# The exchange through DRAM: rows of its blocks at a pitch of 5 KB

## The chip, the cores and the metric

The kernel runs on one core of a Trainium2 chip. The core has a matrix engine (TensorE, PE in the profile, with its weight loads as PEld), a vector engine (VectorE, DVE), a scalar engine (ScalarE, ACT), GpSimd (POOL) and SyncE (SP), which here does nothing but issue DMAs. Sixteen DMA engines move data between DRAM (HBM) and the on-chip memory SBUF, which has 128 partitions. The metric is the device time of one execution in microseconds, as the median of several runs; lower is better.

## What is computed

One block of a transformer with a mixture of experts, in float32: 16 sequences of 256 tokens, 256 features, 16 heads of 64, and 8 experts with 1024 hidden units. Cut to what matters:

```python
shift = silu(t) @ W_ada.T + b_ada
h = _ln(x, ln1_g, ln1_b) + shift
qkv = (h @ Wqkv.T).reshape(b, n, 3, H, HD)
q = _ln(qkv[:, :, 0].transpose(0, 2, 1, 3), qn_g, qn_b)
k = _ln(qkv[:, :, 1].transpose(0, 2, 1, 3), kn_g, kn_b)
v = qkv[:, :, 2].transpose(0, 2, 1, 3)
attn = softmax(einsum('bhnd,bhmd->bhnm', q, k) / sqrt(HD), axis=-1)
o = einsum('bhnm,bhmd->bhnd', attn, v).transpose(0, 2, 1, 3).reshape(b, n, H * HD)
x = x + o @ Wout.T
tok = x.reshape(-1, d)
gate = softmax(tok @ Wgate.T, axis=-1)
vals, idx = top_k(gate.T, tok.shape[0] // E)      # each expert takes 512 tokens
g = _ln(tok[idx.T.reshape(-1)], mlp_g, mlp_b).reshape(-1, E, d)
y = gelu(einsum('ked,ehd->keh', g, fc1s) + b1s)
y = (einsum('keh,edh->ked', y, fc2s) + b2s) * vals.T[..., None]
tok = tok.at[idx.T.reshape(-1)].add(y.reshape(-1, d))
```

## The kernel before

The attention part goes through the 16 sequences one after another, with the work of neighbours overlapped. For each sequence the class `First` (L632) normalises x and turns it, and `Group` (L676) multiplies it with `wqkvT` in six groups of 512 columns for each half of 128 tokens. Groups 0 and 1 are queries, 2 and 3 keys, 4 and 5 values. `Quad` (L796) is the attention of four heads in two pairs (index `i`): scores, row maxima, exponentials with row sums, division by the sums, and the product with v. `Tail` (L918) projects with `woutT`, adds x, stores the tokens and their normalised form, and works out the gate. After the last sequences comes the routing and then the expert part (`Job`, L1190), which loads 2 MB of weights for each job.

Two things have to be transposed so that the contraction lies on the partitions: queries and keys (tokens on the partitions when they come out of the matmul, head features wanted there), and the probabilities (queries on the partitions, keys wanted). For the first and the last sequence (`DIRECT`, L171) TensorE transposes. For the fourteen others it is done by an exchange through DRAM, in four steps:

- `turn` (L751 for queries and keys, L846 for probabilities): VectorE transposes blocks of 32 x 32 in place, within each group of 32 partitions, into a tile of 128 partitions x 1024 floats (`kb` or `pb`, 4 KB in each partition).
- `away` (L759 and L856): one DMA on SP's queue writes the whole tile, 512 KB, to a tile in DRAM named `kblocks` or `blocks`, shape [4, 32, 4, 256], the row of 4 KB of each partition after that of the partition before. All these DRAM tiles share four buffers (`bufs=4`).
- `back` (L766 and L869): four DMAs on SP's queue read it, `q` = 0 to 3. Read `q` takes from each of the 128 rows the piece of 1 KB at place `q`, and writes 32 partitions of SBUF, four pieces into each: for probabilities to `prT`, for queries to `qraw`, for keys to `kT`.
- The consumer: ScalarE's `affine` (L777) applies gain and bias to queries (L781) and keys (L789), on which the scores (L813) wait; the product with v (L900) reads `prT` directly.

For a sequence with the exchange that makes 12 stores (four of queries and keys, eight of probabilities) and 48 reads.

The order of the instructions on every engine and on SP's queue is not found at run time. `Plan` (L45) collects steps, and a list of numbers written out by hand, `PLACES` (L182), sorts them; `PERIOD` (L173) is the distance of two sequences in those numbers, 48.3. A step that waits for a semaphore holds up everything behind it on the same engine. On SP, in particular, a `back` waits for the landing of its `away`, and later DMAs stand behind it. The durations given with the steps (`took`, `lag`) are notes; the order is that of `PLACES`.

Of the kernel before, what the change touches and what calls it, by code (L numbers as in the profile page):

```python
# [9 lines left out]
F32 = mybir.dt.float32  # L10
# [9 lines left out]
B, N, D = 16, 256, 256  # L20
# [14 lines left out]
SQ = 32  # L35
QB = P // SQ
# [28 lines left out]
def kernel(  # L65
# [17 lines left out]
    dram = ctx.enter_context(tc.tile_pool(name="dram", bufs=1, space=DRAM))  # L83
# [444 lines left out]
    if True:  # L528
# [147 lines left out]
        class Group:  # L676
# [80 lines left out]
                )  # L757

            def away(self, kb):  # L759
                self.blocks = dram.tile([QB, SQ, QB, N], F32, tag="blocks", bufs=4, name="kblocks")  # L760
                nc.sync.dma_start(
                    self.blocks.rearrange("k d q n -> (k d) (q n)"),
                    kb[0].rearrange("p q t h m -> p (q t h m)"),
                )

# [30 lines left out]
        class Quad:  # L796
# [58 lines left out]

            def away(self, i):  # L856

                self.blocks[i] = dram.tile([QB, SQ, QB, N], F32, tag="blocks", bufs=4, name="blocks")
                nc.sync.dma_start(
                    self.blocks[i].rearrange("k m q n -> (k m) (q n)"),  # L860
                    self.pb[i].rearrange("p q c h t n -> p (q c h t n)"),
                )

# [486 lines left out]
        for b in range(B):  # L1350
# [16 lines left out]
            for (g, t), p in GROUP.items():  # L1367
                p += base
                a = Group(b, g, t)
                n = (b, g, t)  # L1370
# [3 lines left out]
                if g < 4:  # L1374
# [4 lines left out]
                    if b not in DIRECT:  # L1379
                        kb, blocks = ("pb", b, -1, g), ("blocks", b, -1, g)  # L1380
# [17 lines left out]
            for d in range(HP // 2):  # L1398
# [3 lines left out]
                n = (b, d)  # L1402
                po = ("po", 0) + n
                for i in range(2):
                    q = p + 3 * i
                    m = n + (i,)
                    sums, pb, prT, blocks = ("sums",) + m, ("pb",) + m, ("prT",) + m, ("blocks",) + m
# [20 lines left out]
            for t in range(TB):  # L1428
                a = Tail(b, t)
                p = base + TAIL[t]  # L1430
                n = (b, t)
# [55 lines left out]
        for n in range(2):  # L1487
            a = jobs[n]
            k = top + 10 + 20 * n
# [4 lines left out]
            for i in range(6):  # L1494
                name, took, by = {"D": ("DVE", 0.81, nc.vector), "P": ("POOL", 1.4, nc.gpsimd), "A": ("ACT", 3.5, nc.scalar)}[who[i]]
# [13 lines left out]
        k = top + 30  # L1509
# [36 lines left out]
        for k in range(1, len(jobs)):  # L1546
# [4 lines left out]
            for s in range(SLOTS):  # L1551
# [28 lines left out]
                else:  # L1580
                    i, q = divmod(s - FC, 4)
# [56 lines left out]
```

## Time and profile before

| | |
|---|---|
| median of 3 runs | 1095.7 us (1095.66 to 1098.27) |
| profiled execution | 1098.53 us, its span 1096.8 us |
| TensorE busy | 1050.9 us (96% of the span) |
| VectorE busy | 809.8 us (74%) |
| GpSimd busy | 615.8 us (56%) |
| ScalarE busy | 591.5 us (54%) |
| DMA traffic | 238.56 MB in 167,700 packets |
| granted TensorE clock | 0.992 of full speed on average |

The span is the time from the first to the last instruction of the profiled execution. Busy times leave out register, branch, semaphore and DMA-issuing instructions. A line of a group or a wait names the engine, the tile that is written and the source line; "A <- B" means that A stood idle until B released it. Matmuls are pipelined, so the busy time of TensorE counts some overlapped time, and some of its stalls are not seen as idle. The DMA share is the time that packets took, summed over the 16 engines and divided by 16 times the length of the stretch; packets in flight can overlap on an engine, so it can be a little over 1. The attention part lasts until about 800 us and the routing and expert part from there to the end.

### The profile page before, as it was taken

The numbers are of one execution on the slowest core, as the hardware profiler recorded it, in microseconds if no ns is written. First come the engines' busy times: TensorE is split into PE (matmuls) and PEld (weight loads), VectorE is DVE, ScalarE is ACT, GpSimd is POOL, SyncE is SP. The second block draws the span as 40 slices with busy tenths as digits, with TensorE's granted clock in tenths as the row PEclk, the third lists the DMA queues.
The fourth block names the chain that finished last, engine by engine and source line by source line (L and its number), as shares of the span: only waits on it lengthen the run. The fifth ranks groups of instructions, "written<-read, shape, count | busy, mean of one in ns | idle before, by whom it ended". The sixth has DMA issues, their size and how long they took to land. (4 is left out here: it accounts for less than half of the span.)

```text
span 1096.8 us, 18716 instructions
## 1 busy us (share of the span) xinstructions
PE 1050.9 (96%) x5611; PEld 685.9 (63%) x5611; DVE 809.8 (74%) x2257; ACT 591.5 (54%) x1656; POOL 615.8 (56%) x997
## 2 busy tenths in 40 slices
PE   6999999999999999999999999999988999999996
PEld 3555646556454645555565555656667888888885
DVE  6667878888887797887888788875579488655540
ACT  1768666666665655666666557675622323332331
POOL 3766766678667585666667676665411333333332
PEclk8999999999999999999999999999999999999998
DMA  6026989999998999998999999986120456565661
GB/s 213 1 77 188 273 261 294 285 281 261 282 278 269 282 280 284 283 286 255 281 294 275 285 283 266 310 265 186 64 101 20 132 172 202 169 174 171 194 202 19
DMA packets 167700, 238.56 MB, mean 218 GB/s; under 512 B 17328, under 2 KB 139440, under 8 KB 167600
## 3 DMA queue, kind: packets, MB, share of 16 engines
q1 hardware_dynamic: 159680, 227.08, 70.2%
q0 software_dynamic: 6144, 8.39, 4.2%
q10 hardware_dynamic: 1776, 1.90, 0.5%
q8 instruction: 45, 0.74, 0.3%
q14 instruction: 55, 0.45, 0.2%
HBM read 136.64 MB, written 100.66 MB: 216 GB/s over the span
## 5 line engine op out<-in xcount | busy, mean ns | idle before, releaser
L688 PE MATMUL pm<-wq,hT 128*128 128x512 f32 x768 | 361.5, 606 | 13.1 <-DVE qk L721 6.3
L841 POOL TENSOR_SCALAR pr<-pr,sums 128x256 f32<-128x256 f32 x512 | 237.0, 481 | 107.3 <-DVE sums L837 99.5
L830 ACT ACTIVATE pr<-sc,nmax 128x256 f32<-128x256 f32 x512 | 237.3, 481 | 98.3 <-DVE nmax L821 78.6
L688 PEld LDWEIGHTS pm<-wq,hT 128*128 128x128 f32 x768 | 136.8, 190 | 168.1 <-issue 131.6
L103 POOL TENSOR_TENSOR ss<-ss,neghalf 128x8 f32<-128x8 f32 x128 | 211.0, 1648 | 10.6
L821 DVE TENSOR_REDUCE nmax<-sc 128x2 f32<-128x512 f32 x256 | 165.4, 673 | 19.9 <-PE sc L813 19.6
L851 DVE STREAM_TRANSPOSE pb<-pr 128x512 f32<-128x512 f32 x224 | 150.1, 690 | 20.7 <-DMA kblocks<-kb 9.5
L813 PE MATMUL sc<-kT,qT 64*128 64x256 f32 x1024 | 137.4, 396 | 3.5 <-ACT kT L789 3.0
L900 PE MATMUL po<-prT,v 128*64 128x256 f32 x1024 | 129.5, 387 | 2.1 <-DMA prT<-blocks 1.8
L701 ACT ACTIVATE sq<-pm 128x512 f32<-128x512 f32 x128 | 75.8, 604 | 96.1 <-PE pm L688 95.6
L813 PEld LDWEIGHTS sc<-kT,qT 64*128 64x128 f32 x1024 | 91.9, 186 | 52.8 <-issue 26.7
L1319 POOL DMA_INDIRECT out<-y,idx x32 | 51.2, 1599 | 119.1 <-DVE y L1313 65.9
L1286 PE MATMUL ph<-xT,w 128*128 128x256 f32 x512 | 117.8, 383 | 0.0
L1302 PE MATMUL py<-w,hid 128*128 128x256 f32 x512 | 116.3, 380 | 0.0
L926 PE MATMUL pw<-wo,oT 128*128 128x256 f32 x512 | 115.3, 382 | 0.0
L926 PEld LDWEIGHTS pw<-wo,oT 128*128 128x128 f32 x512 | 96.2, 190 | 20.9 <-issue 6.0
L830 ACT ACTIVATION_READ_ACCUMULATOR pr<-sc,nmax 128x1 f32 x512 | 109.0, 213 | 0.0
L900 PEld LDWEIGHTS po<-prT,v 128*64 128x64 f32 x1024 | 66.8, 136 | 67.1 <-issue 23.7
L705 DVE TENSOR_REDUCE ss<-sq 128x8 f32<-128x512 f32 x128 | 85.1, 671 | 29.1 <-ACT sq L701 28.6
L1293 ACT ACTIVATE hid<-ph,vec 128x256 f32<-128x256 f32 x128 | 60.3, 473 | 84.6 <-PE ph L1286 79.5
L1302 PEld LDWEIGHTS py<-w,hid 128*128 128x128 f32 x512 | 95.6, 190 | 12.8
L1286 PEld LDWEIGHTS ph<-xT,w 128*128 128x128 f32 x512 | 95.4, 190 | 12.8
(141 smaller groups left out, 1096.1 us busy)
## 6 DMA issues: line engine op xcount, KB each, us to landing
blocks<-pb SPq DMA_DIRECT2D x112, 512.0 KB, 5.0
prT<-blocks SPq DMA_DIRECT2D x448, 128.0 KB, 4.3
kblocks<-kb SPq DMA_DIRECT2D x56, 512.0 KB, 4.3
w<-in_fc2T SPq DMA_DIRECT2D x16, 1024.0 KB, 5.7
w<-in_fc1T SPq DMA_DIRECT2D x16, 1024.0 KB, 8.3
qraw<-kblocks SPq DMA_DIRECT2D x112, 128.0 KB, 4.0
kT<-kblocks SPq DMA_DIRECT2D x112, 128.0 KB, 4.2
out<-tok SPq DMA_DIRECT2D x32, 128.0 KB, 4.1
```

The lines of the kernel that those rows point to most:

```text
L103: nc.gpsimd.tensor_tensor(dst, src, neghalf[:, : src.shape[1]], ALU.pow)
L688: nc.tensor.matmul(self.pm, hTs[self.b][:, c, bass.ts(self.t, P)], wq[:, c, bass.ts(self.g, GW)], start=(c == 0), stop=(c == DC - 1),)
L705: nc.vector.tensor_reduce(self.ss[:, 0, :], self.sq.rearrange("p (h d) -> p h d", d=HD), AX.X, ALU.add,)
L813: nc.tensor.matmul(self.sc[i, j][:, t, :], qTs[self.b][rows, hp, bass.ts(t, P)], keys[rows, hp] if direct else keys[rows, hp // 4, hp % 4] ...
L821: nc.vector.tensor_reduce(self.nmax[i, j], self.sc[i, j], AX.X, ALU.max, negate=True)
L830: nc.scalar.activation(self.pr[i, j][:, t, :], self.sc[i, j][:, t, :], AF.Exp, bias=self.nmax[i, j][:, t : t + 1], scale=1.0, accum_out=se ...
L841: nc.gpsimd.tensor_scalar(self.pr[i, j][:, t, :], self.pr[i, j][:, t, :], self.sums[i][:, 1, j, t : t + 1], 1.0, ALU.mult, ALU.mult,)
L851: nc.vector.transpose(self.pb[i][:, :, :, j].rearrange("p k c t n -> p t k c n"), self.pr[i, j].rearrange("p t (k c m) -> p t k c m", c=TB ...
L900: nc.tensor.matmul(self.po[j * HD : (j + 1) * HD, i, :], vs[self.b][:, c, bass.ts(4 * self.d + 2 * i + j, HD)], prT[:, j, c] if self.b in ...
L926: nc.tensor.matmul(self.pw, oTs[self.b][:, hp // 2, self.t, hp % 2, :], wo[:, hp, :], start=(hp == 0), stop=(hp == HP - 1),)
L1286: nc.tensor.matmul(self.ph[f], self.w1[:, c, bass.ts(f, P)], self.xT[:, c, :], start=(c == 0), stop=(c == DC - 1),)
L1302: nc.tensor.matmul(self.py[i], self.hid[:, f, bass.ts(i, P)], self.w2[:, f, :], start=(f == 0), stop=(f == FC - 1),)
```

## The change

The DRAM tiles of the exchange get one more place along their third axis, five places of 256 floats where there were four. The stores write the first four, and the reads take the first four, as before. So the row of each partition still has 4 KB of data, but rows start 5 KB apart and the last 1 KB of each is never written or read. A tile takes 640 KB of DRAM rather than 512 KB. `back` is not touched: it indexes places 0 to 3 of the wider tile.

```diff
             def away(self, kb):
-                self.blocks = dram.tile([QB, SQ, QB, N], F32, tag="blocks", bufs=4, name="kblocks")
+                self.blocks = dram.tile([QB, SQ, QB + 1, N], F32, tag="blocks", bufs=4, name="kblocks")
                 nc.sync.dma_start(
-                    self.blocks.rearrange("k d q n -> (k d) (q n)"),
+                    self.blocks[:, :, :QB].rearrange("k d q n -> (k d) (q n)"),
                     kb[0].rearrange("p q t h m -> p (q t h m)"),
                 )
...
             def away(self, i):
 
-                self.blocks[i] = dram.tile([QB, SQ, QB, N], F32, tag="blocks", bufs=4, name="blocks")
+                self.blocks[i] = dram.tile([QB, SQ, QB + 1, N], F32, tag="blocks", bufs=4, name="blocks")
                 nc.sync.dma_start(
-                    self.blocks[i].rearrange("k m q n -> (k m) (q n)"),
+                    self.blocks[i][:, :, :QB].rearrange("k m q n -> (k m) (q n)"),
                     self.pb[i].rearrange("p q c h t n -> p (q c h t n)"),
                 )
```

## The prediction

> **What bounds the kernel now.** I read the page first, for the share of each engine, then the stretches of one period each, then the waits of TensorE and ScalarE, and last short stretches in which the DMA engines did one kind of work.
>
> The page's busy times, slices and DMA part:
>
> ```profile
> span 1096.8 us, 18716 instructions
> PE 1050.9 (96%) x5611; PEld 685.9 (63%) x5611; DVE 809.8 (74%) x2257; ACT 591.5 (54%) x1656; POOL 615.8 (56%) x997
> ...
> PE   6999999999999999999999999999988999999996
> ...
> DMA  6026989999998999998999999986120456565661
> ...
> q1 hardware_dynamic: 159680, 227.08, 70.2%
> ...
> blocks<-pb SPq DMA_DIRECT2D x112, 512.0 KB, 5.0
> prT<-blocks SPq DMA_DIRECT2D x448, 128.0 KB, 4.3
> kblocks<-kb SPq DMA_DIRECT2D x56, 512.0 KB, 4.3
> ```
>
> The reader is to see two rows of nines: TensorE from the second slice on, and the DMA engines in slices 5 to 26, which is the attention part. The exchange through DRAM (the last three lines, with the reads into qraw and kT) is most of the traffic: 168 stores of 512 KB and 672 reads of 128 KB, 88 MB each way, 176 of the 227 MB of the SP queue.
>
> One period (the work of one sequence) takes 48.2 us: the output projections of sequence 1 begin at 117.8 us and those of sequence 14 at 744.7, thirteen periods later. Stretches of about one period, with TensorE's busy time, its clock, the share of the 16 DMA engines and the rate:
>
> ```profile
> 158.00:206.00 48.00, 47.43 (x224) 1.00 0.96 276
> 302.00:350.00 48.00, 46.89 (x220) 1.00 0.93 268
> 446.00:494.00 48.00, 45.61 (x224) 1.00 1.02 289
> 638.00:686.00 48.00, 47.44 (x239) 1.00 1.00 284
> ```
>
> Thirteen such stretches, from 110 to 734 us, give a mean DMA share of 0.978 and 608.0 us of TensorE busy in 624. So both are nearly full, TensorE at full clock, and only 16.0 us of TensorE's idle time are left to win there. Where TensorE or its weight loads wait there for the exchange, it shows in these rows (total us, times, longest):
>
> ```profile
> PE sc L813 <- ACT kT L789: 3.0, 3, 1.9
> PE po L900 <- DMA prT<-blocks: 1.8, 3, 1.4
> ...
> PEld sc L813 <- ACT kT L789: 5.0, 4, 2.3
> PEld sc L813 <- ACT qT L781: 2.7, 4, 0.8
> ...
> ACT kT L789 <- DMA kT<-kblocks: 18.4, 16, 2.0
> ACT qT L781 <- DMA qraw<-kblocks: 11.7, 10, 2.3
> ```
>
> ScalarE waits for the reads of keys and queries for 30.1 us in all, and about 13.3 us of that reaches TensorE: 3.0 + 1.8 + 5.0 + 2.7, and 0.8 us of weight loads that wait for prT directly.
>
> **The change, part by part.** No instruction is added or removed; nothing moves on any queue. Per period there are still 12 stores (away, L759 and L856) and 12 groups of four reads (back, L766 and L869). Sizes stay: the trace's packet records show stores in packets of 4096 bytes and reads in packets of 1024, and each row of 4 KB and each piece of 1 KB stays contiguous. What changes is addresses: rows start every 5 KB, so the 128 pieces of one read, which all sat at the same offset within 4 KB, now step through all four offsets. A tile grows from 512 to 640 KB of DRAM, which nothing waits for.
>
> Issue. A store's DRAM side was one run of 512 KB and is now 128 rows with gaps, so its issue could cost more. A store issues in 338 to 376 ns (medians of the two lines), a read, with one more dimension, in 430. At worst 92 ns x 12 = 1.1 us of SP per period, and at best nothing. SP stands waiting 61.0 us for stores of probabilities to land in 110 to 734 us, 4.7 us a period, which covers it. I take 0; without the cover it would be 13 x 1.1 = 14 us at most.
>
> The reads. Three stretches, each with one kind of transfer only (columns: busy of the engines, clock, DMA share, GB/s):
>
> ```profile
> 335.00:339.00 4.00, 4.00 (x23) 1.94 (x23) 3.97 (x8) 1.95 (x3) 1.55 (x3) 1.00 1.11 221
> 341.50:343.00 1.50, 1.50 (x9) 0.69 (x9) 0.18 (x1) 0.98 (x4) 1.50 (x4) 1.00 1.05 429
> 891.50:893.00 1.50, 1.50 (x9) 1.32 (x8) 1.50 (x10) 0.74 (x2) 0.54 (x1) 1.00 1.08 373
> 7.00:12.00 5.00, 4.62 (x24) 3.83 (x25) 3.88 (x10) 1.02 (x2) 0.74 (x2) 0.60 1.05 391
> ```
>
> The first is reads of the exchange alone: engines full, yet 221 GB/s. The second is stores alone: 429. The third is the expert weights fc2T, also 1 KB pieces, but rows that follow each other in DRAM and 128 partitions to land in: 373. The fourth is mostly wqkvT, 2 KB pieces at a pitch of 12 KB, into 128 partitions: 391. In the packet records a 1 KB packet takes 46 ns undisturbed; the exchange's reads average 69 ns, with two peaks, at 46 and about 80. In the same stage the reads of x (1 KB pieces, rows without gaps) average 59.
>
> So the exchange's reads go at 0.6 of the rate of their like, and they differ in two ways: the common offset at a pitch of 4 KB, and that each lands in only 32 partitions. The trace has no transfer with one of the two alone. The pitch of 12 KB in the fourth row speaks for the partitions; that the reads slow down only as a group goes on (first of four 63 ns, last 75) fits either.
>
> Bounds: at one end the partitions are all, and the saving is 0. At the other the pitch is all: 69 to 46 ns, which is 32 packets per engine and group x 23 ns = 0.74 us a group, and 13.3 us and more of TensorE's waits go, at most the 16.0 us that are there. Below nothing I leave open too: see the third rival. I take the row nearest in place, queue and packet size, the reads of x at 59 ns: 32 x 10 ns = 0.32 us a group. Groups queue behind one another (at 332 to 338 us SP issues three in a row), so the landing that is waited for moves by 0.32 to 0.64 us, mean 0.48. ScalarE's waits for kT have a mean of 18.4/16 = 1.15 us; 0.48/1.15 = 0.42 of 13.3 us is 5.5 us. The profiled execution took 1098.5 us (span 1096.8), 0.26% above the median of 1095.7; from its own time the sum gives 1093.0, from the median 1090.2. With 48 x 128 packets x 10 ns / 16 = 3.8 us less of DMA work per period, the DMA share would fall from 0.98 to about 0.90, and what is late next is TensorE itself, and ScalarE's wait for the row maxima (68.0 us in the same stretch), which the change doesn't touch.
>
> [...]
>
> The stores. Alone they run at 429 GB/s; a gap behind each row could cost nothing, or bring them to the next lower row of full engines, 373 (15% more). I take nothing, since each packet still writes 4096 bytes in one run; the other end goes into the range.
>
> **The rivals.**
>
> Nothing changes, because the 32 partitions set the rate. For it: 221 GB/s held for 4 us on end, and the 391 at a pitch of 12 KB. Against it: the first packets of a group run at 250 GB/s and more. Time 1095.7, give or take the 0.3% (3.3 us) that a measurement of this kernel can tell from no change.
>
> The pitch is all. Reads go at 46 ns, the exchange costs 8.8 us less of DMA time per period, and all of TensorE's visible idle time goes: 1095.7 - 16.0 = 1079.7. Against it stands that TensorE is then the only bound, and that its order is written out by hand for the present landings. I count it with the forecast, as the far end of the same case.
>
> Slower: the stores lose. Twelve stores are 12 x 128 packets x 159 ns / 16 = 15.3 us of DMA time in each 48.2 us. The free share is 1 - 0.978, 1.05 us a period, so from 7% slower stores on the DMA queue falls behind, every read behind a store lands late, and TensorE waits. At 15% it is 2.3 us more, 1.2 over the slack, 13 x 1.2 = 16 us: 1112. For it: the share has no room, and SP waits for stores to land more than for anything else (61.0 us, and 27.4 for those of keys and queries). Against it: the packet's size and its run are as before.
>
> **How the numbers follow.** Faster by over 0.3%: 0.41, own range 1079 to 1092, forecast 1090. No change that shows: 0.29. Slower: 0.30, of which about a third beyond 1108, and a little of the faster case below 1078. That is the range, 1078 to 1108.
>
> **What the profile after would show.** Right: reads of the exchange alone above 240 GB/s where 221 stood, the median landing of prT at 4.0 us or less, the DMA share of the periods near 0.90, and ScalarE's waits for kT and qT at two thirds or less of 30.1 us. Right on the stores: packets of 4096 bytes and 159 ns, and a landing of 5.0 us or less. Wrong: reads still at about 220 and landings at 4.3 (the partitions hold them), or stores below 400 GB/s with SP waiting more for them (the slower case). A store issue above 430 ns would mean that the gaps cost SP time after all.

## The result, and the profile after

The change makes the kernel slightly faster: 1091.3 us (median of 7 runs, 1088.47 to 1093.01) against 1096.6 us (7 runs, 1095.13 to 1098.85), a ratio of 0.9947 with a 95% interval of 0.993 to 0.9964. By the ratio that is 5.8 us; the two medians differ by 5.3. The profiled execution took 1091.3 us, with a span of 1089.5.

The page of the kernel after, its busy times, the slices of the DMA engines, the SP queue's row, and the landings (out and in, KB of one, median us from issue to landing):

```profile
span 1089.5 us, 18716 instructions
PE 1050.4 (96%) x5611; PEld 686.6 (63%) x5611; DVE 809.4 (74%) x2257; ACT 592.3 (54%) x1656; POOL 617.5 (57%) x997
...
DMA  6025899999999999998999999985130556655661
...
q1 hardware_dynamic: 159680, 227.08, 69.9%
...
blocks<-pb SPq DMA_DIRECT2D x112, 512.0 KB, 4.7
prT<-blocks SPq DMA_DIRECT2D x448, 128.0 KB, 4.1
kblocks<-kb SPq DMA_DIRECT2D x56, 512.0 KB, 4.1
```

The work is the same: as many instructions, the same busy time of TensorE (1050.9 before), the same number of packets and bytes in the queue. What differs is the landings: the reads into prT land 0.2 us sooner in the median, and the stores 0.2 to 0.3. The four periods shown for the kernel before, in the kernel after (TensorE's busy time, its clock, DMA share, GB/s):

```profile
158.00:206.00 48.00, 47.87 (x230) 1.00 0.98 286
302.00:350.00 48.00, 48.00 (x230) 1.00 0.94 278
446.00:494.00 48.00, 46.53 (x248) 1.00 1.03 292
638.00:686.00 48.00, 47.18 (x242) 1.00 0.97 284
```

The DMA engines are as full as before, and TensorE has fewer gaps in three of the four. Over the whole attention stretch, 110 to 734 us (the columns are the length, the busy time of PE, PEld, DVE, ACT and POOL, the clock, the DMA share and GB/s), first in the kernel before and then in the kernel after:

```profile
110.00:734.00 624.00, 607.98 (x2951) 345.35 (x2950) 520.97 (x1040) 399.26 (x1189) 427.74 (x741) 1.00 0.98 279
```

```profile
110.00:734.00 624.00, 614.80 (x2986) 348.66 (x2986) 526.60 (x1052) 408.11 (x1213) 434.13 (x754) 1.00 0.98 283
```

TensorE's idle time in these 624 us falls from 16.0 to 9.2 us. Where it came from shows in the waits of the same stretch (total us, times, longest). In the kernel before, one row of them that the prediction gives as a number only is

```profile
PEld po L900 <- DMA prT<-blocks: 0.8, 1, 0.8
```

and in the kernel after the rows are

```profile
ACT kT L789 <- DMA kT<-kblocks: 12.3, 13, 1.9
ACT qT L781 <- DMA qraw<-kblocks: 8.9, 8, 3.0
...
PEld sc L813 <- ACT kT L789: 2.2, 3, 1.0
...
PEld po L900 <- DMA prT<-blocks: 1.4, 3, 0.8
PE po L900 <- DMA prT<-blocks: 1.3, 1, 1.3
...
PEld sc L813 <- ACT qT L781: 0.8, 1, 0.8
...
PE sc L813 <- ACT kT L789: 0.6, 1, 0.6
```

The five rows of TensorE and its weight loads held 13.3 us before and hold 6.3 now, 7.0 less, about what the idle time lost. ScalarE's waits for the reads of keys and queries fell from 30.1 to 21.2 us. The two profiled executions differ by 7.2 us, so these rows show a little more than the 5.8 of all runs. The gain is therefore where it was forecast, in reads of the exchange that land a little sooner. The experiments ask why they do.

### The profile page after: what moved, and what is told of

Read it like the earlier page. It is cut to its first block, busy times and chain, and to the rows that moved or that the text cites. A ratio compares the mean times of both kernels' runs of the same rounds, so it can differ in the third digit from the quotient of the medians.

```text
span 1089.5 us, 18716 instructions
## 1 busy us (share of the span) xinstructions
PE 1050.4 (96%) x5611; PEld 686.6 (63%) x5611; DVE 809.4 (74%) x2257; ACT 592.3 (54%) x1656; POOL 617.5 (57%) x997
```

## The experiments

Four theories are tried. A: the addresses hold the reads back, since all pieces of a read lie at the same offset within 4 KB. B: the 32 partitions into which a read lands hold it back, and the pitch does little. C: the pitch costs only a group of reads that starts on a quiet queue, not a full queue. D: it is the stores that gain. The runs came in three sets, each on a chip of its own, with its own runs of the kernel before (medians 1098.1, 1099.8 and 1094.7 us), and every ratio is to those.

### Stores and reads by themselves

A kernel that has only transfers: stores of 512 KB and groups of four reads as in the exchange, without the rest of the computation. Its output is x. The sections differ in the pitch alone.

```python
tiles = {k: [dram.tile([QB, SQ, w, N], F32, ...) for i in range(4)]
         for k, w in {"four": 4, "five": 5, "six": 6, "eight": 8}.items()}
tiles["byplace"] = [dram.tile([QB, QB, SQ, N], F32, ...) ...]       # pieces of 1 KB side by side
...
def narrow(kind, i, j):                                             # as in the exchange
    for q in range(QB):
        nc.sync.dma_start(to[bass.ts(q, SQ)], piece(kind, i, q).rearrange("k d n -> d k n"))
def wide(kind, i, j):                                               # 128 partitions
    for q in range(QB):
        nc.sync.dma_start(to[:, q], piece(kind, i, q).rearrange("k d n -> (k d) n"))
```

> Only the exchange's transfers, in sections that each do one thing, twice over: reads of four 1 KB places from tiles with rows at 4, 5, 6 and 8 KB and from tiles stored place by place (pieces at a pitch of 1 KB), into 32 partitions (narrow) or 128 (wide); stores alone; single groups that wait for their landing; stores and reads mixed. All the rest of the computation is left out, and the output is x. If the common offset at 4 KB holds the reads (theory A): narrow reads at 4 and 8 KB about 221 GB/s, at 5 KB 250 or more, 6 KB between, and wide reads at 4 KB well below wide reads at 5 KB. If the 32 partitions hold them (theory B): all narrow reads 215 to 230 GB/s whatever the pitch, place by place too, and wide reads 290 or more (what SP can issue) at every pitch. The gain of 5 KB then has to show in the mixed sections or in the landing of single groups: there 5 KB is quicker by 3 to 8%.

Eight groups of reads in a row, in a full queue, with rows at 4, 5, 6 and 8 KB and then with the pieces of one place side by side (one row each, in this order; columns: length, busy DVE and POOL, clock, DMA share, GB/s); the last two rows are reads into 128 partitions at 4 and 5 KB:

```profile
48.00:60.00 12.00, 0.85 (x5) 0.00 (x0) 1.00 1.13 230
64.00:78.00 14.00, 1.03 (x6) 0.00 (x0) 1.00 1.13 228
82.00:96.00 14.00, 1.03 (x6) 0.00 (x0) 1.00 1.13 227
100.00:114.00 14.00, 1.08 (x7) 0.00 (x0) 1.00 1.13 227
119.00:133.00 14.00, 1.03 (x6) 0.00 (x0) 1.00 1.13 226
139.00:149.00 10.00, 0.86 (x5) 0.00 (x0) 1.00 0.87 259
152.00:164.00 12.00, 1.03 (x6) 0.00 (x0) 1.00 0.92 273
```

In a full queue the narrow reads run at 226 to 230 GB/s whatever the addresses, even with pieces that follow each other without a gap. Theory A falls there. The last rows pass this rate with a DMA share below one: SP issues one of these reads every 474 ns (median), which allows 276 GB/s, so they wait for SP's issue and not for the engines. The 290 that theory B asked for was not reached. Sections that mix 12 stores with 10 groups took 38 to 40.5 us at every pitch, in no order by pitch. One thing differed: six groups, each begun only after the one before had landed, took 29.9 and 30.6 us at 4 KB, and 27.6 and 27.7 at 5 KB. A part of that is the first group, which had other traffic ahead of it; the median group took 4.33 and 4.47 us at 4 KB, 4.05 and 4.06 at 5 KB.

That the 226 to 230 GB/s don't move with the pitch agrees with a limit on the side of the partitions: the last rows, into 128 of them, go at 259 and 273.

### The distance of the tiles without the pitch

With the change a tile of the exchange also grows from 512 to 640 KB. Here it grows and the rows stay at 4 KB:

```diff
-dram.tile([QB, SQ, QB, N], F32, tag="blocks", bufs=4, ...)
+dram.tile([QB + 1, SQ, QB, N], F32, tag="blocks", bufs=4, ...)   # store and reads use [:QB]
```

> Rows at 4 KB as before, but the tile takes 640 KB: the spare 128 KB lie behind it, not behind each row. If the rows' pitch is what counts: ratio to before 0.998 to 1.003. If the distance between tiles (640 KB, not 512 KB) is what counts: 0.993 to 0.997, as with the change.

1098.8 us, ratio 0.9999 (0.9984 to 1.0014). The distance between tiles does nothing; what counts is the pitch of the rows. Its profile is also a second one at a pitch of 4 KB and shows how far two profiles differ by themselves: from 110 to 734 us the five rows of TensorE's waits hold 12.3 us (13.3 in the kernel before), ScalarE's two 30.1 (30.1), and TensorE is idle for 14.7 (16.0). The fall to 6.3, 21.2 and 9.2 is well beyond that.

### A pitch of 8 KB

```diff
-dram.tile([QB, SQ, QB, N], F32, ...)
+dram.tile([QB, SQ, QB + 4, N], F32, ...)
```

> Rows at 8 KB, 4 KB left empty. Theory A (a common offset within 4 KB): no gain, ratio 0.998 to 1.006. If it is any gap, or rows that don't touch, that helps: 0.993 to 0.997.

1113.7 us, ratio 1.0138 (1.0122 to 1.0154): slower than at 4 KB, and outside both expectations. Stores land in 5.1 and 4.7 us and the reads into prT in 4.4. Its waits from 110 to 734 us:

```profile
ACT qT L781 <- DMA qraw<-kblocks: 16.6, 13, 3.7
ACT kT L789 <- DMA kT<-kblocks: 16.5, 13, 1.9
...
PE po L900 <- DMA prT<-blocks: 5.2, 5, 2.4
...
PEld po L900 <- DMA prT<-blocks: 3.5, 3, 2.8
```

The stores and the reads into prT land a little later than at 4 KB, TensorE waits for the probabilities themselves (8.7 us in the last two rows, 2.6 before), and it is busy for 601.2 us of the 624. So a gap behind the rows does not help by being a gap: its size decides.

### Reads into 128 partitions

Rows at 4 KB, but each read takes its 128 pieces to 128 partitions. This leaves out the last step of the transposition, so what is computed is another thing, at the same number of bytes, packets and instructions.

```diff
-raw[bass.ts(q, SQ)], self.blocks[:, :, q].rearrange("k d n -> d k n")
+raw[:, q], self.blocks[:, :, q].rearrange("k d n -> (k d) n")
...
-prT[bass.ts(q, SQ)], self.blocks[i][:, :, q].rearrange("k m n -> m k n")
+prT[:, q], self.blocks[i][:, :, q].rearrange("k m n -> (k m) n")
```

> Rows at 4 KB as before; each read takes the same 128 pieces from DRAM but puts them into 128 partitions, one piece each, rather than four pieces into each of 32. The last step of the transposition is left out by it. Theory A (pitch): reads alone stay near 221 GB/s and the time within 0.5% of before. Theory B (partitions): reads alone at 290 GB/s or more, the DMA share of a period falls from 0.98 below 0.85, and the time falls to 0.98 to 0.99 of before.

1082.8 us, ratio 0.9855 (0.9839 to 0.9872). The stretch from 110 to 734 us (columns as above):

```profile
110.00:734.00 624.00, 620.12 (x3034) 355.03 (x3033) 533.37 (x1063) 412.11 (x1231) 440.76 (x766) 1.00 0.86 287
```

Stores land in 4.2 us and the reads into prT in 3.4. The DMA share falls from 0.98 to 0.86 (below 0.85 was expected), and TensorE's idle time from 16.0 to 3.9 us. This is the picture that the prediction had drawn for the pitch, and it is the partitions that make it, at the old pitch. Theory B holds for the rate of reads: where they land sets it.

### Single groups at ten pitches

A second kernel of transfers alone, with x as output: eight groups of four reads at each pitch, each narrow group begun after the one before has landed, and the whole a second time. "fourquarter" and "fourhalf" are 4.25 and 4.5 KB.

```python
PITCH = {"four": 1024, "fourquarter": 1088, "fourhalf": 1152, "five": 1280, "six": 1536,
         "seven": 1792, "eight": 2048, "nine": 2304, "ten": 2560, "twelve": 3072}   # floats
...
def alternate(kind, i, j):
    narrow(kind, i, j, (0, 2, 1, 3))       # the order of the four places
def alone(kind, read):
    for j in range(8):
        read(kind, j, j)
        settle(dst[j : j + 1])              # the next group waits for this one
```

> Only the exchange's transfers again, now single groups of four reads, each begun when the one before has landed, from rows at 4, 4.25, 4.5, 5, 6, 7, 8, 9, 10 and 12 KB and place by place; the same with wide reads, and with the places in the order 0, 2, 1, 3; single stores. All the rest of the computation is left out, and the output is x. Theory C (the pitch counts only while a group is short of the rate that 32 partitions allow): a group at 4 KB takes 0.3 to 0.5 us longer than at 5 KB, and so do its wide reads; 8 and 12 KB are as slow as 4 KB or slower, since they keep the common offset; 7 and 9 KB are as quick as 5 KB. Theory D (it is the stores that land earlier): groups of reads differ little from pitch to pitch, and a single store at 5 KB lands 0.2 us or more before one at 4 KB. Reads in the order 0, 2, 1, 3, where two that follow each other lie in different halves of the partitions: above 250 GB/s in a full queue if the limit belongs to partitions, 226 if not.

The timeline of the SP queue in the second pass (start, length of the section, out and in; L90 are narrow reads, L100 wide ones):

```profile
755.30 34.56 SPq L90 DMA_DIRECT2D dst<-four  x32
...
863.76 31.96 SPq L90 DMA_DIRECT2D dst<-five  x32
...
967.97 34.18 SPq L90 DMA_DIRECT2D dst<-eight  x32
...
1074.87 33.09 SPq L90 DMA_DIRECT2D dst<-twelve  x32
1110.72 31.77 SPq L90 DMA_DIRECT2D dst<-byplace  x32
1144.93 19.93 SPq L100 DMA_DIRECT2D dst<-four  x32
1165.79 20.25 SPq L100 DMA_DIRECT2D dst<-five  x32
```

The whole section at 4 or 8 KB is longer than at 5 KB by 2 to 3 us; the first group at 4 KB also had other traffic ahead of it, which a median leaves out. By the issues and landings of each group (medians of eight, first and second pass):

| pitch | a group, us | its first read, us |
|---|---|---|
| 4 KB | 4.33, 4.24 | 2.63, 2.51 |
| 4.25 KB | 4.03, 4.08 | |
| 4.5 KB | 4.14, 4.02 | |
| 5 KB | 4.05, 4.01 | 2.37, 2.37 |
| 6 KB | 4.11, 4.05 | |
| 7 KB | 4.05, 4.00 | |
| 8 KB | 4.38, 4.33 | 2.70, 2.70 |
| 9 KB | 4.09, 4.01 | |
| 10 KB | 4.03, 4.04 | |
| 12 KB | 4.07, 4.10 | 2.40, 2.37 |
| pieces side by side | 4.03, 3.99 | |

Only 4 and 8 KB stand out, by 0.24 to 0.33 us a group against 5 KB, and most of it is there when the first of the four reads lands (0.14 to 0.33). The packets don't show it: a packet of 1 KB takes 55.9 and 56.3 ns at 4 KB, 57.0 and 56.2 at 5 KB. At 4 KB the delay therefore lies outside what the packet records time. Theory C is borne out at 8 KB, at 7 and 9 KB, and at 4 KB, there a little below the 0.3 us that it asked for. It misses two points: 12 KB, where the pieces of a read again share one offset within 4 KB, is not slow, so a common offset is not the condition; and wide reads at 4 KB (3.90 and 3.82 us a group) are not slower than at 5 (3.97 and 4.02). At 8 KB wide reads are slower (4.23 and 4.26), so the delay there does not need the 32 partitions. The wide groups overlap: the eight at 4 KB were issued within 19.93 us, so each began before the one ahead of it had landed. In the order 0, 2, 1, 3 of the places a single group took 4.05 and 4.11 us at 4 KB, 3.90 and 3.86 at 5 and 4.23 and 4.17 at 8: order and pitch each take something off.

Does this delay reach the kernel, whose queue is seldom quiet? By the issues and landings in the trace of the kernel before, of its 168 groups of reads three start with no other transfer of SP's queue under way, 11 with one, and 117 with five or more. Each group of the kernel after, set against the same group of the kernel before, takes 0.22 us less on average from its first issue to its last landing (give or take 0.08; 5.95 before). The 117 take 0.25 less (give or take 0.10), and the 14 with none or one take 0.23 less (give or take 0.18). In the kernel with larger tiles at 4 KB the groups differ by 0.02 (give or take 0.08). So something of the size of the single groups' delay goes in the kernel as well, and in its busy queue too, which theory C had left out. The profiles of before and after can be of two chips, so a part of the 0.22 can be the chip's. Why the full queues of reads and the mixed sections above showed no such difference is open.

The stores, one at a time at three pitches, from the page (median us to landing in the last column):

```profile
four<-src SPq DMA_DIRECT2D x20, 512.0 KB, 2.6
five<-src SPq DMA_DIRECT2D x20, 512.0 KB, 2.6
eight<-src SPq DMA_DIRECT2D x20, 512.0 KB, 2.6
```

Theory D falls for a store by itself: 2.60 us at each of the three. That stores land sooner in the kernel after (4.7 against 5.0) would fit their queue, which they share with the reads; no run shows it.

The order of places was a side question: 0, 2, 1, 3 in a full queue, in both passes, each time first at 4 KB and then at 5 KB (columns as in the first such table):

```profile
655.00:670.00 15.00, 0.86 (x5) 0.00 (x0) 1.00 0.98 233
671.00:688.00 17.00, 1.37 (x8) 0.00 (x0) 1.00 1.12 245
1335.00:1350.00 15.00, 1.03 (x6) 0.00 (x0) 1.00 0.92 249
1351.00:1366.00 15.00, 1.35 (x8) 0.00 (x0) 1.00 1.11 252
```

At 5 KB 245 and 252 GB/s stand against 226 to 230 in the order 0, 1, 2, 3 of the first kernel of transfers, which ran on another chip; at 4 KB, where the DMA share stays below one, it is 233 and 249. The number q of a read picks its place in DRAM as well as its 32 partitions, so this order changes both. That the rate moved with no layout in DRAM speaks for the partitions; no run parts the two. This is the larger lever, and the kernel got it next.

### The change with the places in another order

```diff
 # both functions `back`, with the change in place
-for q in range(QB):
+for q in (0, 2, 1, 3):
```

> The change, and the four reads of a group issued in the order 0, 2, 1, 3. If reads that follow each other then use different halves of what the partitions hang on, full queues go faster than 226 GB/s and the ratio to before falls from 0.9947 to 0.985 to 0.992; if each single read of 32 partitions stays bound by itself, 0.993 to 0.997 as with the change.

1084.8 us, ratio 0.9865 (0.9845 to 0.9885): nothing is left out of the computation, and the gain is over twice that of the change. The stretch from 110 to 734 us:

```profile
110.00:734.00 624.00, 617.82 (x3018) 352.67 (x3018) 531.47 (x1058) 410.39 (x1224) 436.74 (x758) 1.00 0.90 285
```

The DMA share is 0.90 and TensorE is idle for 6.2 us. The same bytes now fit into the engines with room to spare. Of the halves that the expectation supposes no run shows anything.

### The order alone

```diff
 # both functions `back`, rows at 4 KB
-for q in range(QB):
+for q in (0, 2, 1, 3):
```

> Rows at 4 KB as before, the four reads of a group in the order 0, 2, 1, 3. With rows at 5 KB this order gave 0.9865. If order and pitch remove the same waits: 0.986 to 0.989. If they add up (the order shortens full queues, the pitch single groups): 0.990 to 0.994.

1084.5 us, ratio 0.9902 (0.988 to 0.9924), with landings of prT at 3.8 us. The stretch from 110 to 734 us has a DMA share of 0.90 as well:

```profile
110.00:734.00 624.00, 618.59 (x3021) 353.98 (x3020) 532.69 (x1060) 410.59 (x1226) 437.68 (x760) 1.00 0.90 286
```

The order thus does most of what the two do together. If they add, the product is 0.9902 x 0.9947 = 0.985, and 0.9865 was measured; but the intervals of 0.9865 and 0.9902 touch and come from two chips, so that they add is not settled. The waits don't settle it either: ScalarE waits for keys and queries for 14.4 us here and for 8.5 with order and pitch, while TensorE is idle for 5.4 and 6.2.

### Wide reads and the new pitch together

```diff
 # the reads of the wide kernel, leaving out the same step, and
+dram.tile([QB, SQ, QB + 1, N], F32, ...)
```

> Rows at 5 KB and reads that put one piece into each of 128 partitions; the last step of the transposition is left out by it. With rows at 4 KB these reads gave 0.9855. If the pitch is worth something of its own also where the partitions don't bind: 0.980 to 0.984. If both remedies take away the same waits: 0.984 to 0.987.

1082.2 us, ratio 0.9847 (0.9826 to 0.9868), against 0.9855 with wide reads at 4 KB: no difference that shows. TensorE's idle time is 3.0 us (3.9 at 4 KB). Where reads are wide, 5 KB in place of 4 is worth nothing, as the single groups said; or there is nothing left to win. Both explain it, and this run can't part them.

### A pitch of 6 KB

```diff
+dram.tile([QB, SQ, QB + 2, N], F32, ...)
```

> Rows at 6 KB: the offset within 4 KB takes two values, not one and not four. Theory A and C: between the kernel before and the change, ratio 0.996 to 1.001. If any gap that is not a multiple of 4 KB does it: 0.993 to 0.997.

1091.7 us, ratio 0.9928 (0.9912 to 0.9943). At 6 KB the pieces of a read use only two of the four offsets within 4 KB, and the gain is as large as at 5 KB (0.9947). So it is not needed that the pieces step through all four offsets, which the prediction had named as what changes.

### A pitch of 12 KB

```diff
+dram.tile([QB, SQ, QB + 8, N], F32, ...)
```

> Rows at 12 KB, 8 KB left empty. The common offset within 4 KB is kept, as at 4 and 8 KB, but 12 is no power of two, and single groups at 12 KB were as quick as at 5 KB. If that is what counts: 0.992 to 0.997. If tiles of 1 MB and more, or the common offset, made 8 KB slow: 1.005 to 1.02.

1093.7 us, ratio 0.9986 (0.997 to 1.0002), between the two expectations, and not clear of no change. The reads into prT land as in the kernel after, at 4.1 us (means 4.09 and 4.07), but those of keys less so: 4.25 in the mean, where the kernel before has 4.38 and the kernel after 4.11. Group by group the reads take 0.11 us less than in the kernel before, half of the 0.22 at 5 KB, and TensorE and its weight loads still wait for 10.3 us in the five rows (2.1 + 1.4 + 4.2 + 1.5 + 1.1), against 6.3 with the change and 13.3 before. Why a pitch that is fast in single groups brings half as much here is open.

### Half of the change: keys and queries, or probabilities

Of twelve groups per period eight are the probabilities' and four those of queries and keys. The pitch is changed in one class alone (the other keeps 4 KB, and the keys' tiles have a tag of their own).

```diff
 # Group.away alone; then Quad.away alone
+dram.tile([QB, SQ, QB + 1, N], F32, ...)
```

> Rows at 5 KB for queries and keys alone (4 of 12 stores a sequence); probabilities stay at 4 KB. Queries and keys now have four DRAM buffers of their own. If the gain comes through the waits for kT and qT, as the prediction's sum had it: 0.995 to 0.998, at least half of the gain. If it goes with the number of groups: 0.998 to 0.999.

> Rows at 5 KB for probabilities alone (8 of 12 stores a sequence); queries and keys stay at 4 KB, in four DRAM buffers of their own. By the prediction's sum, with the waits for kT and qT left: 0.997 to 1.000. If it goes with the number of groups: 0.995 to 0.997.

Keys and queries alone: 1094.6 us, ratio 0.9997 (0.9984 to 1.001), above both expectations, though its interval reaches into one. Probabilities alone: 1092.3 us, ratio 0.9969 (0.9955 to 0.9984), as expected if the gain goes with the number of groups. ScalarE's waits for keys and queries, first with only their own rows moved:

```profile
ACT kT L789 <- DMA kT<-kblocks: 14.2, 14, 2.0
ACT qT L781 <- DMA qraw<-kblocks: 11.2, 8, 2.4
```

and then with only the probabilities' rows moved:

```profile
ACT kT L789 <- DMA kT<-kblocks: 13.0, 13, 2.0
ACT qT L781 <- DMA qraw<-kblocks: 11.3, 10, 2.4
```

These are 25.4 and 24.3 us in all, whichever class was moved; the kernel with rows at 12 KB, from the same set, has 26.0. The reads agree: group by group, against the kernel before, those of probabilities take 0.20 us less in both halves and those of keys and queries 0.10 and 0.11. This would fit a gain that comes through the queue which all of them share. But it isn't shown. The kernel before (30.1 us) was not profiled on this set's chip, on which it is about 2 us faster than in the first comparison, and both halves have eight DRAM buffers where it has four; no run has these buffers alone. The two profiled executions also took the same time, 1093.6 and 1093.7 us, where the medians differ by 2.3. What the ratios do show is that only the half with twice the groups gives a gain that can be seen.

## Why the prediction was right, and where its working was not

The sign and the size hold: 5.5 us forecast, 5.8 measured (5.3 between the medians), and 1091.3 us lies in the range of the faster case, which the prediction gave a chance of 0.41. That the gain comes through reads that land sooner and waits that shorten holds too. The size came out by luck. Step by step:

- **Issue at no cost.** Right. The stores still issue in 338 and 376 ns, and the order of instructions is the same on every engine and on SP's queue.
- **Sizes stay.** Right: stores in packets of 4096 bytes at 159 ns in the median, reads of 1024.
- **The reads' packet term.** Mis-sized, and it was the base of the sum. It put 10 ns on a packet (69 to the 59 of the reads of x). Measured over the exchange's reads, the mean went from 69.0 to 67.3 ns, so 1.7. By 32 packets that is 0.05 us a group, not 0.32.
- **The shift of landings.** Forecast 0.48 us. Whole groups of four land 0.22 us sooner, less than half of it. The means of single reads moved by 0.16 for prT (4.23 to 4.07), 0.27 for kT and 0.10 for qraw (for qraw two kernels at 4 KB differ by 0.09). That is more than the packets explain: with the groups by themselves 0.14 and 0.26 us at 4 KB, against 5 KB, lie before the first read lands, and the packets take the same time. The prediction had no row for that and charged it to packets.
- **From the landings to TensorE.** 0.42 of 13.3 us was worked out, 7.0 us went. The factor was linear in a mean of waits, and the measured shift of a group would have given 0.22/1.15 = 0.19 of 13.3, or 2.5 us. A term over twice too large and a step to the end too small by nearly three times gave the right sum, by luck. Where the missing factor lies is not shown; that landings which come sooner also let SP issue what stands behind them sooner would be one way.
- **The DMA share near 0.90.** Wrong, it stayed at 0.98, and it followed from the packet term. More traffic passed in the same stretch (283 GB/s against 279) at equally full engines. 0.90 and 0.86 came with the other order of places and with 128 partitions.
- **The marks for right.** ScalarE's waits at two thirds or less of 30.1 us: 21.2, or 0.70, just above. The landing of prT at 4.0 or less: 4.1. The DMA share near 0.90: no. Reads alone above 240 GB/s: no; in half-microseconds with hardly anything but reads the median rose by some 2 GB/s and stays near 230, and with transfers by themselves it is 226 to 230 at all pitches. Of these four marks none was met, two nearly. Those for the stores were met (159 ns, 4.7 us).
- **The rival of the partitions.** Right about the rate of reads, wrong only in that this leaves nothing to win. Its evidence, 221 GB/s for 4 us on end, was the better reading than the one that the sum used. The other piece, 391 GB/s at a pitch of 12 KB, was no test of the pitch: into 32 partitions single groups at 12 KB are not slow either.
- **The pitch is all.** Its ratio, 1079.7/1095.7 = 0.985, was reached (0.9847 and 0.9855), but with wide reads and not by the pitch. That TensorE's idle time is what there is to win was sound.
- **The slower rival.** The stores lost nothing: 2.60 us by themselves at 4, 5 and 8 KB, and 4.7 us in the kernel after. A pitch can make the kernel slower all the same (8 KB, 1.4%). Groups of reads by themselves are as slow at 8 KB as at 4 (4.38 against 4.33 us), so by themselves they don't account for it.

Shown by runs: the pitch and not the tiles' distance makes the gain; rows at 4 and 8 KB cost a single group of narrow reads about a quarter of a microsecond, and in the kernel the groups get shorter by nearly as much at 5 KB; the rate in a full queue does not follow the pitch (226 to 230 GB/s), and it follows where the reads land (259 and 273 into 128 partitions) and the order in which they are issued (245 and 252 at 5 KB). Argued: that the shorter groups make the shorter waits of TensorE; it fits the landings, but no run changes the groups' delay alone. Open: what the delay is, since the packets take as long at 4 KB as at 5 (55.9 to 57.0 ns); why it doesn't show in full queues by themselves; where the 1.4% at 8 KB comes from; why 12 KB brings half (0.11 of 0.22 us a group); whether pitch and order add; and how much the chip matters. In the last set the two halves of the change give 0.03% and 0.31%, together 0.34, where the whole gave 0.53% in another set.

## What to carry to other kernels

When reads through DRAM look slow, first part rate and delay, by timing the reads in a full queue and one group at a time: a rate that doesn't move with the addresses points at where the data land (here 226 to 230 GB/s at every pitch, and 259 and 273 into 128 partitions). There the order of destinations is a free lever (here 0, 2, 1, 3 in place of 0, 1, 2, 3: 0.9902 alone, 0.9865 with the pitch), while a pitch of 5 or 6 KB in place of 4 took about a quarter of a microsecond off a group of narrow reads and 0.5 to 0.7% off this kernel. And a forecast of few microseconds can be right by two errors that cancel; look at each term before trusting the next.

## What was not expected of the hardware

- Four reads of 128 KB into 32 partitions each, begun on a quiet queue, take 4.24 to 4.38 us with rows at 4 or 8 KB and 4.00 to 4.14 at eight other pitches from 4.25 to 12 KB, with packets of the same duration at 4 and 5 KB (55.9 to 57.0 ns). Not the offset shared within 4 KB does it, since 12 KB is fast (4.07 and 4.10). Reads into 128 partitions, whose groups overlapped, are slower at 8 KB (4.23 and 4.26 us) but not at 4 (3.90 and 3.82, against 3.97 and 4.02 at 5).
- The order of the four groups of 32 partitions changes the rate of a full queue from 226 to 230 GB/s to 245 to 252 at 5 KB. The order of places in DRAM changes with it, and no run parts the two.
- A pitch of 8 KB makes this kernel 1.4% slower, and a larger tile at a pitch of 4 KB does nothing (0.9999).
